# A gather's lead that shrinks by one tile in twelve instead of five

## The chip, the cores and the metric

The kernel runs on one core of a Trainium2 chip. The metric is the device time of one execution in microseconds (us), as the median of several executions. A core has TensorE (PE in the profile: matmuls; PEld: its weight loads), VectorE (DVE), ScalarE (ACT), GpSimd (POOL) and SyncE (SP). Each engine runs its own list of instructions in order and waits on semaphores for the others. DMAs are issued here from three of these lists: GpSimd's (indirect gathers), SP's and ACT's; sixteen DMA engines carry them out.

## What is computed

One layer of a relational graph network on 12500 nodes with 256 features, 212500 edges sorted by destination, and 8 relations:

```python
h = relu(layernorm(x))
hx = einsum('ni,rio->rno', h, weight)          # 8 relations, 256 x 256 each
agg = segment_sum(hx[edge_type, src], dst)     # over the edges
out = x + agg * 0.5**0.5 + h_bias + (h @ loop_weight) * 0.5**0.5
```

## The kernel before, in words

The kernel turns the order round: it first sums, for every destination node and relation, the rows h[src] of the edges (the sums), and multiplies by the weights afterwards (the products). The edges are cut into 1581 tiles of at most 128. Two tiles make a unit (PAIR = 2), and 128 nodes make a group; a group's 16 products with the weights (line 1187) and two more with loop_weight come after the last unit that may hold one of its edges. Four groups (XG = 4) share a load of x, a load of h and a store.

For each tile, 128 rows of 1 KB are brought from HBM into a buffer `msg`, one row a partition. There are 66 such buffers, given out in pairs (33 pairs in a ring). `edge_sums(t)` (line 985) multiplies the tile's rows by a one-hot matrix that VectorE has made (line 967): four matmuls a tile on TensorE (line 1005). After each unit VectorE adds the result to the ring of sums (line 1031).

The rows come in one of two ways:

- `gather(t)` (line 901) issues one indirect DMA on GpSimd (line 915). The first 100 tiles gather from x, and ScalarE normalises them in place; the other tiles gather from h, which the kernel has written to HBM at its beginning. Each gather is given a dependency on the last unit that had been summed in program order when it was issued ("no faster than the sums", line 919).
- Every 28th tile from 167 on (`single_rows`, line 885: t % 28 = 27), 50 tiles in all, is not gathered. SP and ACT fetch its 128 rows one by one, 64 each, as direct DMAs of 1 KB (`begin_fetch`, line 890; `load_sources`, line 928; the DMA at line 939). The row numbers are loaded into registers, 32 at a time.

The order of work is written out by a Python loop over the tiles (line 1363). In its turn t, it:

- begins the fetch of tile t + 36 (FAR) if that is one of the 50 and the gathers have not yet come so far (line 1365);
- calls `gather` for further tiles until `goal(t)` (lines 1367 to 1369). If `gather` meets one of the 50 tiles at least 36 ahead, it begins that tile's fetch at that point (line 910) and gathers nothing;
- takes at most four entries from each of the two lists of fetches, SP's and ACT's (`fetch`, line 951). A fetch enters the lists eight turns after it was begun (HOLD = 8), and a tile has 66 entries in each list: two loads of registers and 64 rows;
- emits the tile's sums, and, as they come due, pieces of the background work, products and the ends of groups (`finish`, line 1197).

SP's list also holds the loads of x and h (line 1137), the loads of the edges' indices (line 393) and the stores of the result, four groups at a time (line 1206), each at the turn at which the loop emits it. A store waits until VectorE has made the group's result. ACT's list holds, after the beginning, the rows and some small loads (line 405).

`goal(t)` (line 922) says up to which tile the gathers are issued in turn t. The lead is 64 tiles (AHEAD) until tile 170 (NARROW); behind it the lead shrinks by one tile in SLOPE, down to 24 (NEXT). Near the end it shrinks once more, down to 8 (CLOSE). At the beginning it grows by two tiles a tile.

Of the kernel before, what the change touches and what calls it, by code (L numbers as in the profile page):

```python
# [55 lines left out]
STARTED = 24  # L56
STEEP = 2
NARROW = 170
SLOPE = 5
NEXT = 24  # L60
CLOSE = 8

# [182 lines left out]
def kernel(  # L245
# [22 lines left out]
    NT = plan.NT  # L268
# [48 lines left out]
    with ExitStack() as main:  # L317
# [604 lines left out]
        def goal(t):  # L922

            lead = max(NEXT, AHEAD - max(0, t - NARROW) // SLOPE)
            lead = min(lead, max(CLOSE, (NT - t) // SLOPE))
            return min(t + lead + 1, STARTED + STEEP * (t // PAIR * PAIR))

        def load_sources(t, r0, engine):
# [304 lines left out]
        with tc.manual_schedule():  # L1233
# [129 lines left out]
            for t in range(NT):  # L1363
# [3 lines left out]
                while gathered < min(NT, goal(t)):  # L1367
                    gather(gathered)
                    gathered += 1
# [123 lines left out]
```

## Time and profile before

| what | value |
|---|---|
| median of 3 runs | 1983.34 us (1980.15 to 1984.99) |
| the profiled execution, its whole time | 1982.09 us |
| its span, first to last instruction | 1980.4 us |
| its mean granted TensorE clock | 0.949 |
| busy: TensorE / VectorE / GpSimd / ScalarE | 1711.7 / 1309.2 / 1457.9 / 159.2 us |
| gathers: from x / from h | 100 / 1431 |
| rows fetched singly: SP / ACT | 3200 / 3200 |

The profile holds one execution. Its busy times say how long an engine had an instruction in work; the idle time of a group of instructions is the time in which the engine did nothing just before them, put down to what ended it ("issue" if the profile shows nothing that was waited for). Instructions of SP and DMA issues on ACT are not counted as busy; they are seen in the order of time and in the counts of DMA issues.

### The profile page before, as it was taken

Reading aid. Unit: us, or ns where it says so; the run is one execution under the profiler, and the core shown is the slowest. Engines: PE = TensorE matmul, PEld = TensorE weight load, DVE = VectorE, ACT = ScalarE, POOL = GpSimd, SP = SyncE. Lnnn points to the kernel's source line nnn. Section 1 sums busy time; section 2 is a strip of 40 time slices with the busy share of each in tenths; the row PEclk is TensorE's granted clock in tenths of the full one; section 3 lists DMA queues with packets and bytes.
Section 4 is the critical chain, followed back from the end, with each engine's and each line's share of the span. In section 5 each row is a group of like instructions: output and inputs, shape, how many; then the busy total and the mean of one; then the engine's idle time right before and its main releaser. Section 6 shows DMA issues by size and latency. Waiting matters only on the chain. (4 is left out here: it accounts for less than half of the span.)

```text
span 1980.4 us, 41340 instructions
## 1 busy us (share of the span) xinstructions
PE 1711.7 (86%) x10161; PEld 1473.8 (74%) x10161; DVE 1309.2 (66%) x3272; ACT 159.2 (8%) x334; POOL 1457.9 (74%) x1557
## 2 busy tenths in 40 slices
PE   2348999998899888889998898888989989899998
PEld 1247898997777777778777777777777767687897
DVE  6769767886665677656678565578666567665653
ACT  6777200000000000000000000000000000000000
POOL 7677776677777777777777777777777777777774
PEclk8559999999999999999999999999999999999999
DMA  7993444443444444444434444444444344444432
GB/s 252 358 301 103 126 126 134 140 140 107 138 128 122 149 132 120 141 130 121 149 111 141 132 119 143 141 119 141 129 122 142 109 144 130 120 140 125 127 115 78
DMA packets 158363, 279.45 MB, mean 141 GB/s; under 512 B 35376, under 2 KB 109126, under 8 KB 158118
## 3 DMA queue, kind: packets, MB, share of 16 engines
q0 software_dynamic: 73488, 200.77, 34.5%
q1 hardware_dynamic: 76584, 72.73, 11.9%
q10 hardware_dynamic: 8046, 3.30, 0.9%
q8 instruction: 80, 1.31, 0.3%
q14 instruction: 165, 1.35, 0.2%
HBM read 251.06 MB, written 25.60 MB: 140 GB/s over the span
## 5 line engine op out<-in xcount | busy, mean ns | idle before, releaser
L915 POOL DMA_INDIRECT msg<-h,gidx x1431 | 1361.2, 951 | 458.6 <-issue 335.6
L1005 PEld LDWEIGHTS ps<-oh,msg 128*128 128x128 f32 x6324 | 942.1, 198 | 408.1 <-DMA msg<-h,gidx 258.7
L1005 PE MATMUL ps<-oh,msg 128*128 128x136 f32 (+2 forms) x6324 | 1022.8, 291 | 226.3 <-DMA msg<-h,gidx 139.0
L1187 PE MATMUL po<-w,acc 128*128 128x256 f32 x3136 | 891.0, 389 | 15.4 <-DVE acc L1031 15.3
L1031 DVE TENSOR_TENSOR acc<-acc,ps 128x352 f32 x791 | 408.8, 517 | 413.0 <-PE ps L1005 402.1
L1187 PEld LDWEIGHTS po<-w,acc 128*128 128x128 f32 x3136 | 519.0, 193 | 52.1 <-DVE acc L1031 18.6
L1069 DVE SCALAR_TENSOR_TENSOR acc<-types,pt 128x256 f32<-128x256 bf16 (+1 forms) x688 | 247.3, 411 | 67.6 <-PE pt L1051 61.9
L967 DVE TENSOR_TENSOR oh<-fixed,cols 128x544 f32<-128x544 f32 (+1 forms) x396 | 285.8, 722 | 0.0
L915 POOL DMA_INDIRECT msg<-in_x_dram,gidx x100 | 94.8, 948 | 41.4 <-issue 30.1
L1187 PE MATMUL po<-wl,self_t 128*128 128x256 f32 x392 | 115.5, 420 | 3.5 <-DVE acc L1031 1.8
L1187 PEld LDWEIGHTS po<-wl,self_t 128*128 128x128 f32 x392 | 73.8, 210 | 12.6 <-DVE acc L1031 3.1
L853 ACT ACTIVATE msg<-msg,shift,rstd 128x256 f32<-128x256 f32 x100 | 50.8, 586 | 4.4 <-DVE stats L817 3.6
L853 ACT ACTIVATE xt<-xt,shift,rstd 128x256 f32<-128x256 f32 x98 | 50.0, 587 | 7.0 <-DVE shift L850 6.1
L809 DVE BATCH_NORM_STATS2 stats<-xt 128x6 f32<-128x256 f32 x98 | 34.3, 412 | 23.5 <-DMA xt<-in_x_dram 22.7
L1200 DVE TENSOR_TENSOR xr<-xr,po 128x256 f32<-128x256 f32 x98 | 40.4, 412 | 13.4 <-PE po L1187 12.2
L1123 DVE CAST types<-pt 128x512 bf16<-128x512 f32 x22 | 15.2, 691 | 49.6 <-PE pt L1119 49.6
L1056 DVE COPY self_t<-pt 128x256 f32<-128x256 f32 x98 | 40.7, 415 | 8.5 <-PE pt L1051 5.4
L1051 PE MATMUL pt<-ident,hr 128*128 128x128 f32 x196 | 38.9, 281 | 7.2 <-DMA hr<-h 5.3
L442 DVE TENSOR_SCALAR moves<-fixed 128x271 int32<-128x271 int32 (+1 forms) x90 | 40.6, 452 | 4.4 <-DVE acc L1031 3.0
L1201 DVE TENSOR_TENSOR xr<-xr,po 128x256 f32<-128x256 f32 x98 | 41.2, 421 | 3.4
L444 DVE COPY_PREDICATED fixed<-moves,fixed 128x311 int32<-128x311 int32 (+14 forms) x90 | 38.0, 422 | 3.1
L1051 PEld LDWEIGHTS pt<-ident,hr 128*128 128x128 f32 x196 | 25.6, 153 | 10.6 <-DMA hr<-h 5.6
(162 smaller groups left out, 349.1 us busy)
## 6 DMA issues: line engine op xcount, KB each, us to landing
msg<-h ACTq DMA_DIRECT2D x3200, 1.0 KB
msg<-h SPq DMA_DIRECT2D x3200, 1.0 KB
msg<-h,gidx POOLq DMA_INDIRECT x1431
xt<-in_x_dram SPq DMA_DIRECT2D x24, 512.0 KB
h<-xt SPq DMA_DIRECT2D x24, 512.0 KB
xr<-in_x_dram SPq DMA_DIRECT2D x24, 512.0 KB
hr<-h SPq DMA_DIRECT2D x24, 512.0 KB
out_dram<-xr SPq DMA_DIRECT2D x24, 512.0 KB
```

The source lines that it names most:

```text
L442: nc.vector.tensor_single_scalar(m, packed[:, :n], 1 << (bit + k), op=ALU.bitwise_and)
L853: nc.scalar.activation(row, row, AF.Relu, bias=shift[:n, j : j + 1], scale=rstd[:n, j : j + 1])
L915: i = nc.gpsimd.indirect_dma_start(out=msg[t], out_offset=None, in_=table[:, :], in_offset=bass.IndirectOffsetOnAxis(ap=gidx[b][:, at : at ...
L967: j = nc.vector.tensor_tensor(o[:, k : k + v, :i, :width], iota_f[:, :width].unsqueeze(1).unsqueeze(1).to_broadcast([P, v, i, width]), of. ...
L1005: j = nc.tensor.matmul(ps[:, c, first : first + width], m[:, c * P : (c + 1) * P], o[:, :width], start=(i == 0 and c == 0), stop=(end and ...
L1031: i = nc.vector.tensor_tensor(a, a, ps, op=ALU.add)
L1051: in_run("turns", nc.tensor.transpose(pst[:, c, :n], rows_[:n, c * P : (c + 1) * P], ident[:n, :n]), c == KC - 1)
L1056: nc.vector.tensor_copy(got["self", g][:, :, :n], pst[:, :, :n])
L1069: i = nc.vector.scalar_tensor_tensor(acc[:, :, r, s0 : s0 + n], of, float(r + 1), pst[:, :, :n], op0=ALU.is_equal, op1=ALU.mult)
L1187: i = nc.tensor.matmul(got["out", g][:n], lhs, rhs, start=(r == R and c == 0), stop=(r == R - 1 and c == KC - 1))
L1200: nc.vector.tensor_add(rows_[:n, k, :], rows_[:n, k, :], outs[g % 2][:n, 1, :])
L1201: nc.vector.tensor_add(rows_[:n, k, :], rows_[:n, k, :], got["out", g][:n])
```

## The change

The one constant SLOPE had two uses in `goal`: the narrowing behind tile 170, and the narrowing at the end. The change gives the second use a name of its own, END, with the old value 5, and sets SLOPE to 12. The lead that is allowed behind tile 170 thus goes from 64 to 24 over the tiles 170 to 650, where it went over the tiles 170 to 370. The end is as before.

```diff
 NARROW = 170
-SLOPE = 5
+SLOPE = 12
+END = 5
 NEXT = 24
...
             lead = max(NEXT, AHEAD - max(0, t - NARROW) // SLOPE)
-            lead = min(lead, max(CLOSE, (NT - t) // SLOPE))
+            lead = min(lead, max(CLOSE, (NT - t) // END))
             return min(t + lead + 1, STARTED + STEEP * (t // PAIR * PAIR))
```

`goal` decides in which turn a gather is issued, and with it the unit that the gather depends on. Through `gathered` it also decides whether one of the 50 fetched tiles is begun by `gather` or by line 1365.

## The prediction

> **What bounds the kernel now.** I read the page's busy line and its costliest groups first, then GpSimd's groups stretch by stretch, then the counts of gathers and sums up to four moments, and last what the SP and ACT queues issue.
>
> ```profile
> span 1980.4 us, 41340 instructions
> PE 1711.7 (86%) x10161; PEld 1473.8 (74%) x10161; DVE 1309.2 (66%) x3272; ACT 159.2 (8%) x334; POOL 1457.9 (74%) x1557
> L915 POOL DMA_INDIRECT msg<-h,gidx x1431 | 1361.2, 951 | 458.6 <-issue 335.6
> ```
>
> TensorE looks fullest, but GpSimd sets the pace: its group of gathers from h (line 915) has 1361.2 us busy and 458.6 us idle, 1819.8 us in all, and most of that idle time waits for nothing that is shown. The groups of GpSimd by stretch of the span (220:280, 280:360, 409:484, 484:600, 600:1900, in this order; the last figure before the arrows is the idle time before these instructions) say where that idle time is ordinary:
>
> ```profile
> L915 POOL DMA_INDIRECT msg<-h,gidx x49 | 46.4, 948 | 14.9 <-issue 11.6 <-PE ps L1005 2.1 <-DMA msg<-h,gidx 0.9
> L915 POOL DMA_INDIRECT msg<-h,gidx x57 | 54.1, 949 | 25.8 <-issue 13.3 <-DMA msg<-h,gidx 7.7 <-PE ps L1005 4.5
> L915 POOL DMA_INDIRECT msg<-h,gidx x60 | 56.7, 946 | 19.6 <-issue 12.1 <-PE ps L1005 4.1 <-DMA msg<-h,gidx 2.4
> L915 POOL DMA_INDIRECT msg<-h,gidx x89 | 84.5, 949 | 32.3 <-issue 20.5 <-DMA msg<-h,gidx 7.5 <-PE ps L1005 4.3
> L915 POOL DMA_INDIRECT msg<-h,gidx x1033 | 983.7, 952 | 316.3 <-issue 245.5 <-DMA msg<-h,gidx 32.3 <-PE ps L1005 30.8
> ```
>
> From 600 to 1900 us each of 1033 gathers has 316.3/1033 = 0.306 us before it and takes 0.952 us: back to back at 1.258 us. The 0.306 is the gap of an unhindered gather. Take it off elsewhere and the stalls remain: 220:280 none (14.9 - 49 x 0.306 = -0.1); 280:360 25.8 - 57 x 0.306 = 8.4 us; 409:484 19.6 - 60 x 0.306 = 1.2 us; 484:600 32.3 - 89 x 0.306 = 5.1 us. Since GpSimd runs without pause for 1300 us behind them, **every stall up to 600 us is paid at the end**, and TensorE, which is faster, makes nothing of its own up. So the question is what the change does to those stalls.
>
> **Is the lead what holds GpSimd?** The gathers issued and the matmuls of the sums (four a tile) from the start to four moments, two tables of stretches for lines 915 and 1005:
>
> ```profile
> 0.00:300.00 300.00, 212.73 (x225) 0.81 0.66 210
> 0.00:400.00 400.00, 281.70 (x297) 0.85 0.61 192
> 0.00:500.00 500.00, 354.76 (x374) 0.88 0.58 178
> 0.00:600.00 600.00, 427.89 (x451) 0.89 0.56 171
> ```
>
> ```profile
> 0.00:300.00 300.00, 131.03 (x736) 124.51 (x736) 0.81 0.66 210
> 0.00:400.00 400.00, 190.81 (x1144) 183.98 (x1144) 0.85 0.61 192
> 0.00:500.00 500.00, 246.22 (x1501) 237.17 (x1502) 0.88 0.58 178
> 0.00:600.00 600.00, 299.47 (x1831) 284.25 (x1832) 0.89 0.56 171
> ```
>
> Sums stand at tiles 184, 286, 375 and 458; gathers, with the 3, 5, 8 and 11 tiles that SP and ACT fetch (167, 195, 223 ...) counted in, at 228, 302, 382 and 462. GpSimd is thus 44, 16, 7 and 4 tiles ahead. The lead that goal(t) allows at those tiles is 62, 41, 24 and 24. **It is never reached**: TensorE eats the lead because it is faster, not because the rule shrinks it. SLOPE = 12 allows 63, 55, 47 and 40 instead, which releases nobody. Nothing queues behind a new wait on GpSimd, for there is none.
>
> **What does stall GpSimd** is in its order of time (start, duration, idle before it), 280:360 again:
>
> ```profile
> 343.55 0.94 POOL L915 DMA_INDIRECT msg<-h,gidx  x1 [1.34 <-DMA msg<-h,gidx]
> 344.80 0.95 POOL L915 DMA_INDIRECT msg<-h,gidx  x1 [0.31 <-issue]
> 348.14 0.94 POOL L915 DMA_INDIRECT msg<-h,gidx  x1 [0.92 <-DMA msg<-h,gidx]
> ```
>
> The long gaps end with the landing of an earlier gather. The packets of 280:300 by queue (q0 GpSimd's, q10 ACT's, q1 SP's), then the row fetches issued in 280:360, then those in 600:1900:
>
> ```profile
> q0 software_dynamic: 664, 1.80, 31.6%
> q10 hardware_dynamic: 94, 0.05, 1.5%
> q1 hardware_dynamic: 93, 0.05, 1.5%
> ```
>
> ```profile
> msg<-h ACTq DMA_DIRECT2D x192, 1.0 KB
> msg<-h SPq DMA_DIRECT2D x180, 1.0 KB
> ...
> msg<-h SPq DMA_DIRECT2D x2426, 1.0 KB
> msg<-h ACTq DMA_DIRECT2D x2368, 1.0 KB
> ```
>
> The sixteen DMA engines are a third busy on average, so a mean cannot explain late landings. One engine can: a row fetch is one packet of 1 KB and its mark, and if all rows go to one engine, the 3.0% of q1 and q10 are 16 x 3.0 = 48% of it, beside 31.6% of gathers. The completion marks in the trace, which no view prints, agree in kind: fifteen of a gather's sixteen marks come together, the last one late. SP and ACT issued 372 rows in 80 us there, 4.65 a us; in 600:1900 it is 4794/1300 = 3.69 a us, and nothing stalls. [...]
>
> **The change, part by part.** It adds and removes no instruction. The looser bound costs and saves nothing by the leads above. END = 5 keeps the last 120 tiles as they were. What moves is in begin_fetch: a tile t % 28 = 27 that lies inside the allowed lead is begun when the gathers reach it, else 36 tiles ahead. Walking the loop with both slopes, eleven tiles (251 to 531) are begun earlier: 279 from 53 to 60 tiles ahead, 335 from 39 to 55, 391 from 36 to 50, 447 from 36 to 45, 503 from 36 to 40; from 559 on nothing changes. Their 704 rows on each queue move up in program order, past SP's stores, loads of x and h, and loads of indices; GpSimd's own queue keeps its order.
>
> On ACT no store stands between the rows, so its rows go out when the buffer (66 tiles back) is free, as now: 0. On SP a store waits for DVE's result of a group, and the rows behind it wait too. SP's order of time from 370 to 580 us (start, duration), its waits for the two stores at 422 and 498, and the rows that it issued before the stores at 422, 498 and 575:
>
> ```profile
> 376.53 32.42 SPq L939 DMA_DIRECT2D msg<-h  x84
> 422.31 0.42 SPq L1206 DMA_DIRECT2D out_dram<-xr  x1
> ...
> 443.32 42.20 SPq L939 DMA_DIRECT2D msg<-h  x106
> 497.93 0.42 SPq L1206 DMA_DIRECT2D out_dram<-xr  x1
> ...
> 575.49 0.41 SPq L1206 DMA_DIRECT2D out_dram<-xr  x1
> ```
>
> ```profile
> SPq L1206 <- DVE acc L1031: 13.7, 1, 13.7
> SPq L1206 <- DVE acc L1031: 12.7, 1, 12.7
> ```
>
> ```profile
> msg<-h SPq DMA_DIRECT2D x407, 1.0 KB
> msg<-h SPq DMA_DIRECT2D x554, 1.0 KB
> msg<-h SPq DMA_DIRECT2D x704, 1.0 KB
> ```
>
> The stores are emitted at iterations 309, 373 and 435. With the new order (four entries a list and iteration, 66 entries a tile) 448, 576 and 704 rows stand before them: 41 and 22 more, then none. SP's rows now end at 376.53 + 32.42 = 409 and 443.32 + 42.20 = 485.5 us, and it waits. A row takes it 32.42/84 = 0.386 us, so 41 rows are 15.8 us: they **fill the 13.7 us pause at 409 to 422**, in which the crowded engine now catches up. SP and ACT then run full from 230 us until SP has issued 576 rows, at 424 + 128 x 0.386 = 474 us by the mean, some 484 with its loads; I take 484.
>
> - Added: 75 us (409 to 484) at the price of 280:360, where both queues run full against a backlog, 8.4/80 = 0.105 us a us, is 7.9 us; it costs 1.2 now: **+6.7**. Bounds: -1.2 if the stretch costs as little as 220:280 (filling, no stall), +8.1 if it holds to 498 (89 x 0.105 - 1.2). I take the full price: 280:360 is the nearest row with both queues full and a backlog in place.
> - Removed: SP now pauses from 484 to 498 and has 128 rows, not 150, before 575, so part of the 5.1 us of 484:600 goes. Bounds 0 and -5.1; I take half, **-2.5**, because ACT's rows stay and the backlog is full at the start.
> - Delayed: the store at 422 by about 2 us, the load of x at 376 by 47 rows, 18 us. Both are wanted by DVE and TensorE, which wait for GpSimd from 430 us on; if that cover were gone TensorE would wait, and GpSimd, four tiles ahead, would not: 0.
>
> Sum: +4.2 us on the profiled execution of 1982.09 us (span 1980.4 and 1.7 around it): 1986.3. That execution is 1.25 us below the median of the three runs, 1983.34, so **1987.5** for a median.
>
> **Rivals.** First, **nothing moves**: 1983.3. It speaks for it that no instruction changes, that the allowed lead is not reached (so the change does not do what its words say), and that the same rows go to the same engine by 575 us. Against it: stalls depend on when rows come, and a 13.7 us rest vanishes. It holds if the engine serves its queues in turn, so that rows wait for rows and a gather's part for only a row or two. [...]
>
> Second, slower, **the backlog does not drain** in the pause before 498: the full price runs to the store at 575, 166 x 0.105 = 17.4 us, for 1.2 + 5.1 now: +11.1, 1994.4. It decides there: if the last mark still comes late when SP resumes at 499. For it: 484:600 stalls now despite two pauses. Against: 128 SP rows in 77 us are fewer than in any stalled stretch.
>
> Third, faster: **the waits for the sums are real holds** after all. GpSimd's group and waits in 250:600:
>
> ```profile
> L915 POOL DMA_INDIRECT msg<-h,gidx x265 | 251.5, 949 | 99.4 <-issue 58.7 <-DMA msg<-h,gidx 22.3 <-PE ps L1005 16.8
> ```
>
> ```profile
> POOL msg L915 <- PE ps L1005: 16.8, 40, 1.4
> ```
>
> Put down to TensorE are 16.8 - 40 x 0.306 = 4.6 us, 1978.7 if they go; all stalls are 99.4 - 265 x 0.306 = 18.3 us, 1965.0 at the utmost. Against: the leads 44, 16, 7 and 4.
>
> **How the numbers follow.** This kernel's measurement tells about 0.3% from no change, here 6 us: 1977.4 and 1989.3 are the borders. The forecast (rows fill the pause) has 0.62, by itself from 1983.3 - 1.2 - 5.1 = 1977.0 to 1983.3 + 8.1 = 1991.4: of this 0.02 is faster, 0.35 within, 0.25 slower, as the price is taken from one stretch. Nothing moves: 0.16, all within. The backlog stays: 0.13, slower. Real holds: 0.09, of which 0.06 faster and 0.03 within. Together faster 0.08, within 0.54, slower 0.38. Eight in ten lie between 1979 and 1995: below are most of the holds and the forecast's low end, above the tail of the second rival.
>
> **What would show it.** SP's pause before the store at 422 gone and the next one longer (about 14 to 24 us); the group of GpSimd in 409:484 with some 26 us idle, not 19.6, and in 484:600 nearer to 0.306 a gather; the gathers behind 600 us as now; leads at 300 to 600 us as now or smaller. It is wrong if 409:484 does not change (first rival), if 484:600 grows (second), or if GpSimd's lead at 400 us is well over 16 (third).

## The result and the profile after

| | before | after |
|---|---|---|
| median of 5 runs each | 1984.94 us (1980.15 to 1987.9) | 1993.95 us (1988.33 to 1994.77) |
| ratio, 95% interval | | 1.0043 [1.0022, 1.0063] |
| the profiled execution, and its span | 1982.09, 1980.4 us | 1988.33, 1986.6 us |

The changed kernel is slower by 0.43%, 8.5 us by the ratio (4.4 to 12.5). The profiled execution is the fastest of its five and 6.2 us longer than that of before. Its page, the span and the group of gathers (one line further down in the code now):

```profile
span 1986.6 us, 41346 instructions
...
L916 POOL DMA_INDIRECT msg<-h,gidx x1431 | 1358.9, 950 | 467.0 <-issue 335.5
```

The same 1431 gathers are busy 2.3 us less and idle 8.4 us more (458.6 before): 6.1 of the 6.2 us. So it is GpSimd's idle time again, and the stretches say where. GpSimd's group in 220:280, 280:360, 360:409, 409:484, 484:600 and 600:1900 of the changed kernel:

```profile
L916 POOL DMA_INDIRECT msg<-h,gidx x49 | 46.4, 947 | 15.2 <-issue 11.9 <-PE ps L1006 2.1 <-DMA msg<-h,gidx 0.6
L916 POOL DMA_INDIRECT msg<-h,gidx x57 | 53.9, 946 | 26.4 <-issue 14.6 <-DMA msg<-h,gidx 9.2 <-PE ps L1006 2.5
L916 POOL DMA_INDIRECT msg<-h,gidx x35 | 33.2, 949 | 16.8 <-issue 6.9 <-DMA msg<-h,gidx 6.4 <-PE ps L1006 1.7
L916 POOL DMA_INDIRECT msg<-h,gidx x51 | 48.4, 949 | 27.8 <-DMA msg<-h,gidx 11.6 <-issue 9.7 <-PE ps L1006 4.3
L916 POOL DMA_INDIRECT msg<-h,gidx x93 | 88.5, 952 | 29.3 <-issue 21.1 <-PE ps L1006 3.7 <-DMA msg<-h,gidx 3.3
L916 POOL DMA_INDIRECT msg<-h,gidx x1036 | 984.1, 950 | 317.0 <-issue 245.2 <-DMA msg<-h,gidx 35.4 <-PE ps L1006 26.5
```

The one stretch that the prediction didn't quote of before, 360:409:

```profile
L915 POOL DMA_INDIRECT msg<-h,gidx x37 | 35.3, 954 | 14.9 <-issue 7.6 <-DMA msg<-h,gidx 4.4 <-PE ps L1005 2.7
```

Less 0.306 us a gather, as in the prediction, the stalls are (before, after): 280:360 8.4 and 9.0; 360:409 3.6 and 6.1; **409:484 1.2 and 12.2**; 484:600 5.1 and 0.8. That is +0.6, +2.5, +11.0 and -4.3, together +9.8 us. Counted otherwise: 444 gathers are done at 600 us, and 451 were before; seven gathers of 1.258 us are 8.8 us. Behind 600 us a gather still has 317.0/1036 = 0.306 us before it. (There it also took 950 ns and not 952, which gave three gathers or 3.8 us back in this execution; a kernel with the old order of rows, below, has 948, so this isn't the change's doing. 8.8 less 3.8 is, within a gather, the 6.2 us of the two spans, and 8.8 is nearer to the medians' 9.0.)

In 409:484 the word behind most of the idle time has changed as well: it was "issue", now it is "DMA msg<-h,gidx" with 11.6 us, the landing of an earlier gather. What SP did there, from its order of time of 370 to 620 us and its waits:

```profile
398.49 31.15 SPq L940 DMA_DIRECT2D msg<-h  x78
429.75 0.43 SPq L1207 DMA_DIRECT2D out_dram<-xr  x1
434.58 23.28 SPq L940 DMA_DIRECT2D msg<-h  x62
458.42 26.66 SPq L940 DMA_DIRECT2D msg<-h  x66
508.17 0.42 SPq L1207 DMA_DIRECT2D out_dram<-xr  x1
```

```profile
SPq L1207 <- DVE acc L1032: 23.4, 1, 23.4
SPq L1207 <- DVE xr L1202: 18.8, 1, 18.8
```

SP's rows run on until 398.49 + 31.15 = 429.6 us, and the store goes out 0.1 us later: the pause of 13.7 us that stood before it is full of rows. The next rows end at 485.1 us, and the next store waits 23.4 us.

### The profile page after: what moved, and what is told of

Read it like the earlier page. It is cut to its first block, busy times and chain, and to the rows that moved or that the text cites. A ratio compares the mean times of both kernels' runs of the same rounds, so it can differ in the third digit from the quotient of the medians.

```text
span 1986.6 us, 41346 instructions
## 1 busy us (share of the span) xinstructions
PE 1714.1 (86%) x10161; PEld 1471.5 (74%) x10161; DVE 1310.0 (66%) x3272; ACT 159.2 (8%) x334; POOL 1455.5 (73%) x1557
## 3 DMA queue, kind: packets, MB, share of 16 engines
q10 hardware_dynamic: 8046, 3.30, 0.9%
## 5 line engine op out<-in xcount | busy, mean ns | idle before, releaser
L1006 PEld LDWEIGHTS ps<-oh,msg 128*128 128x128 f32 x6324 | 940.4, 198 | 424.5 <-DMA msg<-h,gidx 272.7
```

Source lines behind the costliest of these rows:

```text
L1006: j = nc.tensor.matmul(ps[:, c, first : first + width], m[:, c * P : (c + 1) * P], o[:, :width], start=(i == 0 and c == 0), stop=(end and ...
```

## Experiments

The prediction's theory (**crowding**): the wider bound by itself does nothing; it only begins eleven fetches earlier, and their rows fill SP's pause, in which late landings caught up. Its rivals: the bound itself costs or holds something; or the rows have no part in the stalls. Every kernel below was timed beside the kernel before on the same chip.

**On some chips GpSimd isn't the bound.** Two of the four chips on which the experiments ran took 2428 to 2431 us for the kernel before, where the other two took 1981 us, near the 1985 of the first result. From such a chip, of the kernel with the new bound and the old order of rows, the group of gathers on its page, and GpSimd's waits:

```profile
L914 POOL DMA_INDIRECT msg<-h,gidx x1431 | 1361.0, 951 | 901.9 <-issue 337.2
```

```profile
POOL msg L914 <- issue: 373.3, 1147, 3.9
POOL msg L914 <- remote: 270.3, 167, 3.3
POOL msg L914 <- PE ps L1020: 263.4, 174, 8.0
```

GpSimd idles 901.9 us, twice as long as here, and waits 263.4 us for sums (59.3 us in the kernel before). What is slower there is SP. From its order of time in the kernel with the old bound and the new order of rows, on the same chip:

```profile
853.57 46.11 SPq L954 DMA_DIRECT2D msg<-h  x73
```

A row takes SP 46.11/73 = 0.63 us there, where it took 0.386 here, and on the page of the kernel quoted first 28% of the chain that ended last are SP's row fetches (L954). In all eight kernels that ran on these chips the median time from one row of SP to its next, in 600:1900, is 0.61 to 0.69 us, and 0.32 in the six other profiles; for ACT it is 0.32 to 0.33 in all of them. Why SP is slower there isn't known. (These traces hold 10700 to 11900 landing marks of DMAs, and the others over 39000, so what they call "remote" may well be waits for landings.) Runs from these two chips say nothing on this change; they are told, and no weight is put on them.

### Bound and order of rows apart

Both orders are written into one kernel: `turns(slope)` walks the loop as the kernel does and lists the turn in which each fetch begins, and `goal` takes its slope separately. The diff is that of the first kernel; in the second the 12 and the 5 of the last lines change places.

```diff
+        def goal(t, slope):
+            lead = max(NEXT, AHEAD - max(0, t - NARROW) // slope)
+            lead = min(lead, max(CLOSE, (NT - t) // 5))
...
+            begins.update(turns(12))
...
-                while gathered < min(NT, goal(t)):
+                for s in [s for s in begins if begins[s] == t]:
+                    begin_fetch(s)
+                while gathered < min(NT, goal(t, 5)):
```

**Old bound, new order of rows.** 

> The kernel of e2 again, because in the first four runs the kernel before took 2430 us, not 1985, and GpSimd did not set the pace there. If the kernel before takes some 1985 us beside it. Crowding theory: 8.5 us slower (ratio 1.0043), SP's pause before the store near 422 us gone, GpSimd's stalls in 409:484 about 12 us. Hold theory: as before, within 3 us. If the kernel before takes 2430 us again: no difference, as in e2.

Measured: 1994.6 us, and 1980.77 for the kernel before, ratio **1.0065 [1.0051, 1.0078]**. The slowdown is there without the change's bound. GpSimd's group of this kernel in 280:360, 409:484, 484:510 and 510:600, and SP's stores and rows around the pause:

```profile
L914 POOL DMA_INDIRECT msg<-h,gidx x59 | 55.7, 945 | 26.2 <-issue 13.1 <-DMA msg<-h,gidx 9.1 <-PE ps L1020 4.0
L914 POOL DMA_INDIRECT msg<-h,gidx x51 | 48.5, 950 | 27.0 <-DMA msg<-h,gidx 12.5 <-issue 10.4 <-PE ps L1020 3.2
L914 POOL DMA_INDIRECT msg<-h,gidx x19 | 18.0, 945 | 12.0 <-DMA msg<-h,gidx 8.0 <-issue 4.0
L914 POOL DMA_INDIRECT msg<-h,gidx x72 | 68.4, 949 | 22.0 <-issue 16.5 <-DMA msg<-h,gidx 3.4 <-PE ps L1020 1.2
```

```profile
400.47 31.30 SPq L954 DMA_DIRECT2D msg<-h  x78
431.88 0.42 SPq L1221 DMA_DIRECT2D out_dram<-xr  x1
...
460.67 27.22 SPq L954 DMA_DIRECT2D msg<-h  x66
...
516.87 0.42 SPq L1221 DMA_DIRECT2D out_dram<-xr  x1
```

The pause is gone as in the changed kernel (431.77, store at 431.88), and 409:484 stalls 27.0 - 51 x 0.306 = 11.4 us. This execution goes on stalling in 484:510, 12.0 - 19 x 0.306 = 6.2 us, and then not at all (22.0 - 72 x 0.306 = 0.0). SP's rows before that pause end at 460.67 + 27.22 = 487.9 us, so the backlog takes up to some 22 us of the pause to drain. The profile of the changed kernel is of its fastest run, 3.5 to 6.4 us below the other four; this one, with a whole time of 1994.07 us, may be what the four look like, but that is argued, not shown.

**New bound, old order of rows.** 

> The wide bound of the changed kernel with the fetch turns of the kernel before: SP and ACT get their rows in the old order. Crowding theory (the rows that come earlier and fill SP's pause do the harm): the time of the kernel before within 3 us, SP pausing about 14 us ahead of its store at about 422 us, and the gathers of 409 to 484 us with about 19 to 20 us idle for some 59 of them. Bound theory (the wider bound by itself costs it, GpSimd then waiting elsewhere): as slow as the changed kernel, 8 to 9 us over the kernel before, with the idle time of 409 to 484 us near 28 us.

Measured: 1979.93 us, and 1981.5 for the kernel before, ratio **0.9993 [0.9985, 1.0002]**. 409:484 and 484:600 of GpSimd's group, and SP around its pause:

```profile
L914 POOL DMA_INDIRECT msg<-h,gidx x60 | 57.1, 952 | 19.7 <-issue 13.5 <-DMA msg<-h,gidx 3.4 <-PE ps L1020 2.5
L914 POOL DMA_INDIRECT msg<-h,gidx x89 | 84.4, 948 | 32.1 <-issue 20.2 <-DMA msg<-h,gidx 7.8 <-PE ps L1020 2.1
```

```profile
379.16 32.35 SPq L954 DMA_DIRECT2D msg<-h  x84
424.50 0.43 SPq L1221 DMA_DIRECT2D out_dram<-xr  x1
```

The pause is back (411.5 to 424.5), and the stalls are 1.3 and 4.9 us, those of before. The two runs together settle the question: the wider bound does nothing that can be measured, and the order of the rows makes the whole loss.

**The same two kernels, and fetches begun 64 tiles ahead, on a chip where GpSimd isn't the bound.** The third has `begins.update({s: s - 64 ...})` in place of `turns`. In this order:

> The gathers' bound is that of the changed kernel (one tile in twelve), but the fetched tiles are begun in the turns of the kernel before, so SP's and ACT's lists are those of before. Crowding theory (the change acts only through SP's rows, which come earlier and crowd one DMA engine): as before, within 3 us; SP pauses some 13.7 us before the store at 422 us, and GpSimd's stalls in 409:484 are about 1.2 us. Hold theory (the looser bound on the gathers is what costs): 8.5 us slower, as the changed kernel, with SP's pause in place.

> The reverse: the gathers' bound of before (one tile in five), the fetched tiles begun in the turns of the changed kernel. Crowding theory: 8.5 us slower (ratio 1.0043), SP's pause before the store at 422 us gone, GpSimd's stalls in 409:484 about 12 us. Hold theory: as before, within 3 us.

> A larger dose: the bound of before, and every fetched tile begun 64 tiles ahead throughout. Crowding theory: SP pauses for no store until it meets the buffers' limit near 545 us, so both queues stay full for some 70 us longer than in the changed kernel; at the changed kernel's 12.2 us in 409:484 (0.163 us a us) that is 11 us more: 16 to 20 us slower than before. Hold theory: as before, within 3 us. Third possibility, any earlier fetch costs the same once: 8.5 us.

Measured: 1.0012 [0.9987, 1.0037], 1.0013 [0.9992, 1.0033] and 1.0011 [0.9991, 1.0031], beside 2430.54 us. None of the theories was put to the test: that nothing changes where GpSimd isn't the bound fits crowding, but doesn't speak for it. The larger dose wasn't run on the other chips.

### Fewer rows

```diff
-            return (t % SINGLE == SINGLE - 1 and t + 2 * NEAR < NT
+            every = t % SINGLE == SINGLE - 1 if t >= 440 else t >= 167 and (t - 167) % 36 == 0
+            return (every and t + 2 * NEAR < NT
```

> The kernel before with fewer row fetches early on: one tile in 36 instead of one in 28 goes to SP and ACT from tile 167 to 419, and again one in 28 behind. GpSimd has two or three gathers more to do, at 1.258 us each 3 to 4 us. Crowding theory (the rows per microsecond of SP and ACT together decide: 4.65 stalls, 3.69 does not): the rows of 280 to 360 us fall below 3.7 a us, the idle time before a gather there falls towards 0.306 us, some 12 to 18 us of stalls go, and the time is 8 to 15 us shorter than before. Rival (the stalls come from GpSimd's own gathers or from the loads of x and h, not from the rows): no stalls go, and the time is 3 to 4 us longer.

Measured: 1969.45 us, and 1981.5 for the kernel before on the same chip, ratio **0.9943 [0.9926, 0.9959]**, 11.3 us faster than before; its interval lies wholly below that of the changed kernel. GpSimd's group on its page, then in 280:360, 409:484 and 484:600, then the rows issued in 280:360:

```profile
L916 POOL DMA_INDIRECT msg<-h,gidx x1433 | 1360.8, 950 | 444.4 <-issue 343.6
```

```profile
L916 POOL DMA_INDIRECT msg<-h,gidx x63 | 59.6, 945 | 21.5 <-issue 16.1 <-DMA msg<-h,gidx 2.9 <-PE ps L1006 1.8
L916 POOL DMA_INDIRECT msg<-h,gidx x61 | 58.1, 953 | 18.6 <-issue 13.4 <-DMA msg<-h,gidx 2.1 <-PE ps L1006 2.1
L916 POOL DMA_INDIRECT msg<-h,gidx x93 | 88.3, 949 | 28.4 <-issue 22.6 <-DMA msg<-h,gidx 3.0 <-PE ps L1006 2.1
```

```profile
msg<-h ACTq DMA_DIRECT2D x142, 1.0 KB
msg<-h SPq DMA_DIRECT2D x137, 1.0 KB
```

Two gathers more, 279 rows in 80 us (3.5 a us, where before has 372 or 4.65), and the stalls go: 2.2, -0.1 and -0.1 us. From 250 to 600 us before has 18.3 us of stalls, so about 16 us go and 2.5 come back as two gathers of 1.258 us: 13.5 us, and the profiled spans differ by 1980.4 - 1967.5 = 12.9. Rows, not the gathers themselves nor the loads of x and h, make the stalls, in the kernel before too.

### One engine or sixteen

That all rows go to the same DMA engine was the prediction's reason why a third-busy set of engines can be late. Two ways of testing it were tried. First, each row described as four parts of 256 B:

```diff
-                    msg[t][r0 + i : r0 + i + 1, :].bitcast(U8), h32_bytes[:, bass.ds(v, D * 4)])
+                    msg[t][r0 + i : r0 + i + 1, :].bitcast(U8).rearrange("p (k c) -> p k c", k=4),
+                    h32_bytes[:, bass.ds(v, D * 4)].rearrange("p (k c) -> p k c", k=4))
```

> The kernel before with each fetched row described as 4 parts of 256 bytes, same bytes, same number of DMAs, same order. One-engine theory (all rows go to one DMA engine, whose mark is the late one): the rows spread over four engines, none is crowded, GpSimd's stalls in 250:600 (18.3 us) go to under 3 us: 14 to 19 us faster. Rival (it is the number of DMAs in flight or the memory that is crowded, not one engine): no change within 3 us, or slower, as there are four times the packets. If SP and ACT take over 0.45 us for such a row they fall behind, and TensorE waits for rows: slower.

> The kernel of e4 again, for the same reason. If the kernel before takes some 1985 us beside it. One-engine theory: GpSimd's stalls in 250:600 (18.3 us) go to under 3 us, 14 to 19 us faster. Rival (DMAs in flight or the memory are crowded, not one engine): no change within 3 us, or slower. If the kernel before takes 2430 us again: no difference.

Measured: 1.0004 [0.9985, 1.0023] where GpSimd isn't the bound, and 1979.61 us beside 1980.77, 0.9994 [0.9985, 1.0003], where it is. ACT's queue in the second, and 409:484:

```profile
q10 hardware_dynamic: 8046, 3.30, 0.9%
```

```profile
L915 POOL DMA_INDIRECT msg<-h,gidx x58 | 55.2, 951 | 19.8 <-issue 11.6 <-DMA msg<-h,gidx 3.8 <-PE ps L1006 3.2
```

8046 packets and 3.30 MB, as the unchanged rows have: the parts are no packets of their own, and the kernel is the one before once more. The theory wasn't tested: written in this form, the packet count shows that a row isn't spread.

Second, 800 spare transfers of 1 KB on ACT's queue behind every fourth of its rows, from one partition (`line[0:1, : D]`) or from sixteen partitions with 64 B each (`line[0:16, : D // 16]`), to a tensor that nothing reads:

```diff
+                if engine == ACT and i % 4 == 3:
+                    n = len(spares)
+                    e = nc.scalar.dma_start(spare_rows[n : n + 1, :], line[0:1, : D])
```

> The kernel before, with one more DMA on ACT's list behind every fourth row: 1 KB from one partition to a spare place in HBM that nothing reads, 16 more for each fetched tile, 800 in all. One-engine theory (a one-row DMA uses one DMA engine, and all of them the same one): the rows and extras make 3.69 + 0.46 = 4.15 a us behind 600 us, as in 400:600 of the kernel before (831 rows in 200 us), where GpSimd's stalls were 6.6 us in 200 us: 30 to 60 us slower, with GpSimd's gaps ended by landings. Rival (the memory or the number of DMAs): the same as its twin with the extras over sixteen engines.

> The twin: the same 800 extra DMAs of 1 KB at the same places in ACT's list, but each from 16 partitions of 64 bytes, so that it may be cut over sixteen engines. One-engine theory: within 5 us of the kernel before, as the crowded engine gets a sixteenth of each. Rival: 30 to 60 us slower, like its twin.

> The kernel before, with an extra transfer on ACT's queue behind every fourth of its rows: one partition, 1 KB, to a spare tensor in memory that nothing reads, 800 in all. One-engine theory (all one-row transfers go to the same DMA engine, and a gather's last mark waits there): each extra counts as a row, so 600 to 1900 us goes from 3.69 to 4.15 rows a us, where other runs stall; GpSimd's idle time before a gather there rises above 0.306 us, and the time is 30 to 60 us longer. Theory of the sixteen engines together (mean load, or the number of transfers under way): 0.8 MB more of 279 MB changes nothing, within 5 us of before.

> The same 800 extra transfers of 1 KB at the same places of ACT's queue, but from sixteen partitions with 64 bytes each. They are sixteen packets and sixteen marks instead of one and one; the queue's share on another chip says that they take each engine some 0.015 us instead of 0.12 us on one. One-engine theory: at most a sixth of the harm of the other kernel, 0 to 10 us over before. Theory that the number of transfers in the queues, or ACT's issuing, does it: the same harm as the other kernel.

Measured, both pairs on chips where the kernel before takes 2428 to 2429 us: one partition 1.0059 [1.0026, 1.0091] and 1.0059 [1.0036, 1.0082]; sixteen 1.0041 [1.0014, 1.0067] and 0.9995 [0.9968, 1.0022]. The first pair doesn't separate the two, the second does, and 14 us is well short of the 30 to 60 that were expected where gathers set the pace. What the runs do show is the number of packets on ACT's queue, one kernel each:

```profile
q10 hardware_dynamic: 9646, 4.12, 0.7%
```

```profile
q10 hardware_dynamic: 33646, 4.17, 1.2%
```

9646 - 8046 = 1600 is two a transfer, one of data and one mark; 33646 - 8046 = 25600 is 32. A transfer of 1 KB from one partition is one packet and its mark.

That all rows go to the same engine, these runs don't show, but the kept traces bear it out. They have the times of all packets, though not the engine of each. In the kernel before, from 220 to 1900 us and away from the bulk transfers of SP's queue (826 us in all), a row of ACT is under way for 91.5 us and a row of SP for 72.7 us, and both at once for 0.3 us; two engines that don't mind each other would give 91.5 x 72.7/826 = 8.1 us. Sixteen packets of gathers are under way at once for 17.4 us while no row is, and never while one is: in those 163.9 us there are at most fifteen. So the rows of both queues take their turns on one engine, which also has its part of every gather. Which of the sixteen it is, the traces don't show.

The marks say what this does to a gather. In the kernel before, from 220 us on, the fifteenth of its sixteen marks comes 2.76 us after its start (median). How far the sixteenth is behind the fifteenth, as the median in us of the gathers of which the trace has all sixteen (8 to 54 of them in a cell, so single cells scatter):

| kernel | 280:360 | 360:409 | 409:422 | 422:484 | 484:510 |
|---|---|---|---|---|---|
| before | 7.3 | 4.6 | 4.7 | 5.3 | 4.9 |
| changed | 7.5 | 6.2 | 8.5 | 7.0 | 0.2 |
| old bound, new order of rows | 7.5 | 6.1 | 8.6 | 7.4 | 4.7 |
| new bound, old order of rows | 7.7 | 6.0 | 5.8 | 4.5 | 5.4 |
| fewer rows | 2.4 | 1.3 | 0.0 | 0.6 | 0.4 |

This is the backlog of the crowded engine. GpSimd feels it only when it is long: the gathers use eight semaphores in turn (in the trace each of eight has the marks of 191 or 192 of the 1531 gathers), and a gather waits until the one eight before it has landed. In 250:600 of the kernel before, GpSimd stands idle for more than 0.5 us ahead of 26 gathers, and 24 of these start 0.74 to 0.80 us after the last mark of that earlier gather. Eight gathers take 8 x 1.258 = 10.1 us; less 0.76 and 2.76, the last mark may be some 6.5 us late (an estimate from these numbers) before anything is lost.

## Why the prediction was right, and which terms were too small

- **GpSimd bounds, and stalls up to 600 us are paid at the end**: right. 6.1 of 6.2 us of the profiled spans are its idle and busy time.
- **The lead is never reached**: right. The gathers and the sums of the changed kernel from the start to 400 and 600 us (the counts are in the brackets, four matmuls a tile):

```profile
0.00:400.00 400.00, 279.04 (x295) 0.85 0.61 190
0.00:600.00 600.00, 421.28 (x444) 0.89 0.56 169
```

```profile
0.00:400.00 400.00, 191.41 (x1139) 184.84 (x1140) 0.85 0.61 190
0.00:600.00 600.00, 296.31 (x1800) 282.45 (x1800) 0.89 0.56 169
```

  With 5 and 11 fetched tiles, 300 and 455 against 285 and 450: leads of 15 and 5, where 16 and 4 were and 55 and 41 are now allowed. The new bound with the old rows costs nothing (0.9993), so the rival of real holds and the hold theory fall.
- **One engine late while sixteen are a third busy**: right, by the packets and marks of the kept traces: in 280:360 the last of a gather's marks comes 7.3 us behind the fifteenth (median).
- **The rows move before the store and fill the pause**: right in place and size. No pause at 429.75; 23.4 us, in the 14 to 24 that were named, at the next store; 27.8 us of idle time in 409:484, where some 26 were.
- **Added, +6.7: the step that was mis-sized.** It is +11.0, beyond its upper bound of +8.1. The 75 us cost 12.2/75 = 0.163 us a us, not the 0.105 of 280:360. The rate of rows isn't what decides. Rows issued in 422:484 and GpSimd's group there, before and then after:

```profile
msg<-h ACTq DMA_DIRECT2D x151, 1.0 KB
msg<-h SPq DMA_DIRECT2D x143, 1.0 KB
```

```profile
L915 POOL DMA_INDIRECT msg<-h,gidx x50 | 47.3, 946 | 15.9 <-issue 10.1 <-PE ps L1005 3.1 <-DMA msg<-h,gidx 2.1
```

```profile
msg<-h SPq DMA_DIRECT2D x147, 1.0 KB
msg<-h ACTq DMA_DIRECT2D x119, 1.0 KB
```

```profile
L916 POOL DMA_INDIRECT msg<-h,gidx x42 | 39.9, 950 | 23.4 <-DMA msg<-h,gidx 9.8 <-issue 7.1 <-PE ps L1006 4.3
```

  Before, 294 rows (4.7 a us) stall 15.9 - 50 x 0.306 = 0.6 us; after, 266 rows (4.3 a us) stall 10.5. Fewer rows, many times the stall. The kernel with the old bound and the new order of rows issues 294 rows there, exactly as many as before, and GpSimd's group there stalls 23.7 - 42 x 0.306 = 10.8 us:

```profile
L914 POOL DMA_INDIRECT msg<-h,gidx x42 | 40.0, 951 | 23.7 <-DMA msg<-h,gidx 11.6 <-issue 8.3 <-PE ps L1020 3.2
```

  What counts is the backlog that is there when the rows come, and whether a rest has shortened it: the last mark is 4.7 us late in 409:422 before and 8.5 after. 280:360 was a bad row for the price because it is a mean over two kinds of time. Its first and last 20 us:

```profile
L915 POOL DMA_INDIRECT msg<-h,gidx x15 | 14.2, 946 | 7.3 <-issue 4.7 <-PE ps L1005 1.3 <-DMA msg<-h,gidx 1.0
L915 POOL DMA_INDIRECT msg<-h,gidx x13 | 12.3, 945 | 7.4 <-DMA msg<-h,gidx 4.4 <-issue 2.0 <-PE ps L1005 0.9
```

  They stall 2.7 and 3.4 us, 6.1/40 = 0.153 us a us, close to the 0.163; the 40 us between them stall only 2.2. In the changed kernel the backlog stays beyond those 6.5 us from 400 to 480 (medians of 6.9 to 8.0 us in each 20 us), where in 280:360 before it goes from 7.7 down to 4.5 and up again to 8.3.
- **ACT's rows at 0, and nothing ahead of 409 us**: a second miss. The prediction said that ACT's rows go out as now. In 360:409 ACT issues (before, after):

```profile
msg<-h ACTq DMA_DIRECT2D x73, 1.0 KB
```

```profile
msg<-h ACTq DMA_DIRECT2D x108, 1.0 KB
```

  35 rows more, that are missing later (119 in 422:484, where 151 were). With them the stall in 360:409 grows by 2.5 us, a term that the sum lacks; that ACT's rows make it fits the crowding, but was not tried by itself.
- **Removed, -2.5**: -4.3. More went than half, since the pause before 508 is 23.4 us and the 128 rows behind it come to a backlog that is nearly gone (0.2 us in 484:510).
- **Delayed, 0**: the store at 422.31 goes out at 429.75, 7.4 us later and not about 2. No term of the sum above needs it.
- **The sum** of +4.2 is +9.8 by these terms. The forecast of 1987.5 is 6.5 us under the median, which the range to 1995 holds by 1 us. That it does is in part luck: the forecast's own bounds ended at 1991.4, and the range went further for the sake of the second rival. By the borders that the prediction set, 1993.95 is slower, to which it gave 0.38, and not within, to which it gave 0.54. "Nothing moves" falls with the ratio's interval. **The backlog that doesn't drain** came within a microsecond of the time (1994.4), but by another way: it foresaw the full price up to the store at 575, and behind 510 us no stall is left, in the changed kernel (484:600 with 0.8 us in all) as in the one with the old bound. The backlog does drain, and the price before is higher.
- **The condition of the first rival**, a gather's part that waits for only a row or two: not so here. The last mark is 7.3 us late with 4.65 rows a us, and 2.4 with 3.5, while a row takes some 0.09 us (an estimate from the page of before: ACT's queue has 0.9% of sixteen engines' 1980.4 us, for 3200 rows and a few small loads). Whether the engine serves its queues in turn, no run shows.

## What to carry to other kernels

A constant that limits a lead may do its work by something else that is computed from it: look for every place where it decides an order, and walk those lists with both values. A pause of an engine that isn't the bound can be what lets a shared resource catch up (409:484 stalled 1.2 us behind SP's pause of 13.7 us, and 12.2 without it), and a stretch that looks idle is then worth more than the rows that could fill it; price such a stretch by the part of its model in which the backlog stands at its limit, and not by a mean over times with and without one. And where single-row transfers delay the bounding engine, fewer of them can be faster, even if that engine gets the work: one tile in 36 in place of 28, up to tile 419, made two gathers more and 11.3 us less.

## What the runs showed of the hardware that was not expected

- The kernel before takes 1981 us on two of the four chips of the experiments and 2428 to 2431 on the other two, with TensorE's granted clock at 0.88 in a profiled run there, and 0.95 here. The clock alone, 0.95/0.88 = 1.08, is less than 2430/1981 = 1.23; SP's time for a row is 0.61 to 0.69 us there and 0.32 here.
- Whether rows hurt depends on what went before, more than on their rate: 4.7 a us behind a pause of 13.7 us cost 0.6 us in 62, and 4.3 and 4.7 a us without it 10.5 and 10.8.
- By the packets' times all rows that SP and ACT fetch singly run on one of the sixteen engines (a row of each queue under way at once for 0.3 us, where two engines would give 8.1), and of a gather's sixteen marks fifteen come in 2.76 us (median) and one up to 9.6 us later, in the kernel before. GpSimd loses little until that one delays the landing past the start of the gather eight further on: 24 of its 26 gaps of over 0.5 us in 250:600 end 0.74 to 0.80 us after that landing.
- A transfer of 1 KB from one partition leaves one packet of data and one mark (1600 packets for 800 transfers), and a contiguous row described in four parts still does (8046 packets on ACT's queue with and without the parts).
